# A four-layer graph network in one kernel: a transpose and the setup sums moved from TensorE to VectorE, small products issued in larger batches, and a new order of operations

## The chip, the cores and the metric

The kernel runs on one core of one Trainium2 chip. All times are device microseconds (us) of that core for one execution; the span of a profile, from the first to the last instruction, is some 1.8 us shorter than the time of the same execution (2386.3 against 2388.06 for the changed kernel). The median of several executions is quoted with its lowest and highest value. Of all runs in this study one stray execution (5676.19 us, told below) is left out; all others are fast runs, with mean granted clocks from 0.981 to 0.999.

## The reference

The input is 128 graphs of 64 nodes with 512 features, and one weighted 64x64 adjacency matrix per graph. Everything is fp32. Four layers follow, each a residual around a graph layer with a layer norm and a relu ahead of it. Cut to what matters here:

```python
# layer 0: two hypergraph convolutions; H = (adj != 0)
h  = relu(layernorm(x))
m  = relu(conv(h, H, W1) + b1)              # 512 -> 1024
z  = layernorm(m) * gamma + beta
x  = x + (conv(z, H, W2) + b2) + h          # 1024 -> 512
# layer 1: attention with weight tanh(s_i + s_j), then A @ h @ w
# layer 2: q, k, v; weight = adj * exp(q k^T); x += softmax-like mean of v
h  = relu(layernorm(x))
q, k, v = h @ Wq.T + bq, h @ Wk.T + bk, h @ Wv.T + bv
# layer 3: T = row-normalised adj * exp(leaky_relu(s_j + s_i)); K = 3
h  = relu(layernorm(x))
x  = x + relu(h @ Wk[0] + (T h) @ Wk[1] + (T T h) @ Wk[2] + sum(bk))
```

## The kernel before

Two graphs make a tile of 128 rows, and four tiles make a group. There are 16 groups. All of them pass layers 0 and 1 (the first half), then all pass layers 2 and 3 (the second half), because the weights of both halves use the same two buffers (`wa_mem` and `wb_mem`), which are filled anew in between. Large products use seven instead of eight block products (Strassen).

The kernel is not written in the order in which it runs. Each operation is declared with an engine, a cost and the buffers that it reads and writes. A pass at build time then places the operations one by one: of those that could start first, it takes the one with the smallest priority. It also chooses the buffer slots. The priorities come from about sixty constants, which had been tuned for exactly these operations and costs.

```python
STRETCH, PERIOD1, PERIOD2 = (2.01, 1.52, 3.8, 3.15), 99.32, 100.99
AT = {"x0": -1000.31, "apart": -0.04, "w1": -1140.59, ...}       # cut
...
if pick is not None and (best is None or (t0, pick.prio) < (best[0], best[1].prio)):
    best = t0, pick
assert best and best[0] < float("inf"), "no operation can go on: too few slots"
```

The setup of layer 0 folds gamma, beta and the mean of the second layer norm into W2. `mm` multiplies all of W2 by two columns, and VectorE then subtracts the spread row from W2 so that z needs no mean taken off:

```python
def mm():
    for c in range(KH):
        nc.tensor.matmul(p.t[0:2, :], gsc[:, c, :], w2_sb[:, c, :], start=(c == 0), stop=(c == KH - 1))
...
for c in range(KH):                        # VectorE: W2 * gamma - mean row
    nc.vector.scalar_tensor_tensor(w2_sb[:, c, :], w2_sb[:, c, :], gb2[:, 0, c:c + 1], pm.t,
                                   op0=ALU.mult, op1=ALU.subtract)
```

Layer 0 scales z by its reciprocal deviation only (`rs`), and GpSimd adds h and b2 to x while this goes on:

```python
nc.gpsimd.tensor_add(xx.t, xx.t, h.t)
nc.gpsimd.tensor_add(xx.t, xx.t, b2_b.t)
...
rs = norm_stats(lambda k, z=z: z.t[:, k * D:(k + 1) * D], 2, [(z, 0), (z, 1)])[1]
nc.scalar.activation(half(), half(), AF.Copy, scale=rs.t)
```

Layer 2 issues a batch of 16 small logits products (64 columns, on halves of the array: the form 128*64 in the trace) as soon as one q tile is there. Layer 3 transposes T on TensorE, copies it on ScalarE, multiplies T by T, and applies both to h, one batch of 16 small products for each tile:

```python
def mt():
    for t in range(T):
        nc.tensor.transpose(quad(pt)[:, t, :], tr.t[:, t, :], ident)
pe(KD * TR, mt, trk, [pt])
act(0.59, lambda: nc.scalar.copy(tt.t[:, :, 0, :], quad(pt)), [pt], [(tt, 0)])
def m2():
    for t in range(T):
        nc.tensor.matmul(quad(p2)[:, t, :], tr.t[:, t, :], tt.t[:, t, 0, :], start=True, stop=True)
...
def lm(h=h, pq=pq, t=t):                   # one call per tile
    for c in range(KD):
        for i, half in enumerate(HALVES):
            nc.tensor.matmul(quad(pq[i])[:, c, :], h.t[half, c * P:(c + 1) * P],
                             tt.t[half, t, :, half], start=True, stop=True)
```

## Time and profile before

| | before |
|---|---|
| median of 4 runs | 2400.38 us (2398.42 to 2402.01) |
| span of the profiled run | 2395.1 us |
| TensorE busy / not busy in it | 2356.3 / 38.8 us |
| VectorE, ScalarE, GpSimd busy | 1721.2, 1263.5, 938.2 us |
| stretches at half clock ahead of the last 3 us | 2, of 3.4 us each (clock record of the trace) |

The first line of the table held 3 runs when the prediction was made, with a median of 2401.43 us. "Not busy" is the span less TensorE's busy time. The prediction shows the lines of the page and of the windows from which this is read; what matters in them is that TensorE has no work in only 38.8 us of 2395, of which 16.6 us lie in the first 105 us (the head), 9.9 between 1150 and 1300 us (the change of halves) and nearly all of the rest after that.

### The profile page before, as it was taken

The numbers are of one execution on the slowest core, as the hardware profiler recorded it, in microseconds if no ns is written. First come the engines' busy times: TensorE is split into PE (matmuls) and PEld (weight loads), VectorE is DVE, ScalarE is ACT, GpSimd is POOL, SyncE is SP. The second block draws the span as 40 slices with busy tenths as digits, with TensorE's granted clock in tenths as the row PEclk, the third lists the DMA queues.
The fourth block names the chain that finished last, engine by engine and source line by source line (L and its number), as shares of the span: only waits on it lengthen the run. The fifth ranks groups of instructions, "written<-read, shape, count | busy, mean of one in ns | idle before, by whom it ended". The sixth has DMA issues, their size and how long they took to land.

```text
span 2395.1 us, 33543 instructions
## 1 busy us (share of the span) xinstructions
PE 2356.3 (98%) x11930; PEld 1855.0 (77%) x11930; DVE 1721.2 (72%) x3676; ACT 1263.5 (53%) x1754; POOL 938.2 (39%) x1450
## 2 busy tenths in 40 slices
PE   7999999999999999999999999999999999999999
PEld 3576677776777776777778888888888888888887
DVE  7887878787878787877878556666666666666664
ACT  2666565566565566565745445544445444454431
POOL 5234455434455434455344333333333333333321
PEclk9999999999999999999999999999999999999999
DMA  7232222232223222222532232222322222222211
GB/s 242 54 80 47 65 68 71 68 78 51 65 66 73 67 80 52 61 67 77 146 89 62 66 74 55 69 56 58 78 64 60 66 50 71 73 56 64 52 42 36
DMA packets 335928, 168.78 MB, mean 70 GB/s; under 512 B 284688, under 2 KB 290832, under 8 KB 335760
## 3 DMA queue, kind: packets, MB, share of 16 engines
q1 hardware_dynamic: 335760, 166.63, 28.0%
q8 instruction: 94, 1.54, 0.3%
q14 instruction: 74, 0.61, 0.1%
HBM read 64.76 MB, written 34.70 MB: 42 GB/s over the span
## 4 chain that ended last, share of the span: by engine, by line
PE 84%; DVE 6%; DMA 4%; ACT 2%; POOL 2%; issue 2%; SPq 0%; DVEq 0%; POOLq 0%; ACTq 0%
PE ps L595 60%; PE ps L818 11%; PE ps L534 4%; PE ps L936 2%; PE ps L731 2%; PE ps L879 2%; DVE s_s_vu_tt L869 1%; DMA x<-xm 1%; PE ps L844 1%; ACT o L543 1%; DVE bd L854 1%; ACT h L525 1%; POOL u L867 1%; POOL rs L511 1%; DVE st L508 1%
## 5 line engine op out<-in xcount | busy, mean ns | idle before, releaser
L525 ACT ACTIVATE h<-x,nm,rs 128x512 f32<-128x512 f32 x384 | 307.1, 813 | 456.5 <-POOL nm L518 455.3
L595 PE MATMUL ps<-wb_mem,rT_a 128*128 128x256 f32 x2056 | 476.8, 380 | 1.7 <-DVE z_hT L615 0.9
L595 PEld LDWEIGHTS ps<-wb_mem,rT_a 128*128 128x128 f32 x2056 | 386.5, 190 | 74.8 <-issue 20.3
L510 POOL TENSOR_SCALAR rs<-mv 128x1 f32<-128x1 f32 x320 | 101.5, 317 | 534.2 <-DVE mv L509 452.9
L595 PE MATMUL ps<-wb_mem,s_s_vu_tt 128*128 128x256 f32 x1152 | 275.0, 379 | 0.2 <-DVE s_s_vu_tt L587 0.2
L595 PE MATMUL ps<-wb_mem,tmp_mB_s 128*128 128x256 f32 x1152 | 261.3, 379 | 0.2 <-DVE tmp_mB_s L587 0.2
L595 PEld LDWEIGHTS ps<-wb_mem,s_s_vu_tt 128*128 128x128 f32 x1152 | 218.5, 190 | 43.1 <-issue 10.5
L595 PE MATMUL ps<-wb_mem,mT_a 128*128 128x256 f32 x1016 | 240.7, 380 | 1.8 <-ACT u L563 1.3
L595 PEld LDWEIGHTS ps<-wb_mem,tmp_mB_s 128*128 128x128 f32 x1152 | 217.6, 190 | 29.6 <-DVE tmp_mB_s L587 0.6
L595 PE MATMUL ps<-wa_mem,mT_a 128*128 128x512 f32 x512 | 238.0, 593 | 2.1 <-DVE u L567 2.1
L949 POOL TENSOR_TENSOR u<-u,bk_b 128x256 f32<-128x256 f32 x96 | 76.2, 799 | 352.3 <-DVE u L567 292.6
L511 POOL TENSOR_TENSOR rs<-rs,mhalf 128x1 f32<-128x1 f32 x320 | 202.9, 634 | 26.6
L595 PEld LDWEIGHTS ps<-wb_mem,mT_a 128*128 128x128 f32 x1016 | 190.6, 190 | 28.6 <-ACT u L563 1.5
L508 DVE BATCH_NORM_STATS2 st<-x 128x6 f32<-128x512 f32 x256 | 174.1, 680 | 32.4 <-DMA x<-xm 30.8
L595 PE MATMUL ps<-wa_mem,s_s_vu_tt 128*128 128x512 f32 x384 | 182.9, 599 | 1.0 <-ACT c_b L453 0.6
L595 PEld LDWEIGHTS ps<-wa_mem,mT_a 128*128 128x128 f32 x512 | 96.0, 190 | 105.4 <-issue 92.5
L565 DVE TENSOR_TENSOR u<-ps,u 128x256 f32<-128x256 f32 (+1 forms) x160 | 84.4, 527 | 112.1 <-PE ps L595 84.6
L623 POOL TENSOR_TENSOR u<-u,row_sh_q 128x256 f32<-128x256 f32 x96 | 70.9, 746 | 235.0 <-DVE u L565 205.9
L545 ACT COPY rT_a<-z_hT 128x1024 uint16<-128x1024 uint16 x128 | 144.3, 1161 | 4.4 <-DMA z_hT<-tmp_mB_s 4.2
L534 PEld LDWEIGHTS ps<-bd,h 128*128 128x128 f32 x1024 | 129.0, 192 | 16.1 <-issue 8.6
L707 ACT ACTIVATE z_hT<-z_hT 128x512 f32<-128x512 f32 x128 | 79.8, 625 | 116.7 <-DVE z_hT L615 116.6
L563 ACT COPY u<-ps 128x256 f32<-128x256 f32 (+1 forms) x160 | 72.5, 453 | 129.7 <-PE ps L818 71.5
(172 smaller groups left out, 4317.1 us busy)
## 6 DMA issues: line engine op xcount, KB each, us to landing
x<-in_x_dram SPq DMA_DIRECT2D x64, 256.0 KB, 2.8
xm<-x SPq DMA_DIRECT2D x64, 256.0 KB, 2.0
x<-xm SPq DMA_DIRECT2D x64, 256.0 KB, 2.7
out_dram<-x SPq DMA_DIRECT2D x64, 256.0 KB, 2.2
adj<-in_adj_dram SPq DMA_DIRECT2D x32, 256.0 KB, 4.1
rw<-row SPq DMA_DIRECT2D x96, 64.0 KB, 2.8
wb_mem<-in_Wk_dram SPq DMA_DIRECT2D x6, 512.0 KB, 4.4
wa_mem<-in_W1T_dram SPq DMA_DIRECT2D x2, 1024.0 KB, 5.9
```

What stands on the lines that cost most here:

```text
L508: dve(0.69, lambda i=i: nc.vector.bn_stats(st.t[:, i, :], src(i)), [r[i]], [(st, i)])
L510: pool(0.3, lambda: nc.gpsimd.tensor_scalar_add(rs.t, mv.t[:, 1:2], EPS), [mv], [rs])
L511: pool(0.65, lambda: nc.gpsimd.tensor_tensor(rs.t, rs.t, mhalf, ALU.pow), [rs], [rs])
L525: act(0.82, lambda: nc.scalar.activation(h.t, xx.t, AF.Relu, bias=nm.t, scale=rs.t), [xx, nm, rs], [h])
L534: nc.tensor.matmul(quad(p)[:, c, :], h.t[:, c * P:(c + 1) * P], rhs(), start=True, stop=True)
L545: act(1.16, lambda: nc.scalar.copy(u16(dst()).rearrange("p c (k q) -> p c k q", q=2), u16(back()).rearrange("p (q c r) -> p c r q", q=2, c ...
L563: act(n / 1200 + 0.17, lambda: nc.scalar.copy(at(0)(), p1.t[:, :n]), [p1], [(U, 0)])
L565: dve(c_v(n), lambda: nc.vector.tensor_add(at(1)(), p2.t[:, :n], at(0)()), [p2, (U, 0)], [(U, 1)])
L595: nc.tensor.matmul(p.t[:, :n], lhs()[:, c, :], rhs(c), start=first and c == 0, stop=c == kc - 1, skip_group_check=True)
L707: act(0.63, lambda: nc.scalar.activation(z.t[:, cols], z.t[:, cols], AF.Relu), [(z, j)], [(z, j)])
L818: nc.tensor.matmul(pair(p.t)[:, o, :], a, b, start=first and o == 0 and c == 0, stop=c == 1, skip_group_check=True)
L949: pool(0.88, lambda: nc.gpsimd.tensor_add(U.t[:, iv], U.t[:, u[1]], add()), [u, ka], [v])
```

## The change

Its intent is to take work from TensorE, the engine that is busy 98% of the time, and to issue its smallest products in fewer, larger batches. The parts: (1) VectorE transposes T in blocks of 32x32, so the product that needs T^T has 64 instead of 128 columns; (2) logits are issued for two q tiles at once, and the products with T for two tiles at once; (3) W2 is no longer centred, and what was left of the sums in the setup is done by VectorE, with one product with ones at the end to add over the partitions; ScalarE scales W2 by gamma; (4) z is centred instead, by a bias operand of the same ScalarE operation that scales it, for which GpSimd works out an offset; (5) the layer-3 setup holds fewer temporaries at once, and all priorities are new. The diff cut to its core:

```diff
-    STRETCH, PERIOD1, PERIOD2 = (2.01, 1.52, 3.8, 3.15), 99.32, 100.99
+    STRETCH, PERIOD1, PERIOD2 = (2.14, 5.22, 3.19, 0.39), 82.22, 140.0      # and all of AT
     def setup_l0():
-        pe(c_mm(512, KH), mm, ["gsc0", "gsc1", *wkeys("w2", 0, KH)], [p])   # mm, two spreads,
-        ...                                                                 # W2 * gamma - row
+        for c in range(KH):                                                 # c == 0: tensor_scalar
+                dve(0.77, lambda c=c: nc.vector.scalar_tensor_tensor(
+                    acc.t, w2_sb[:, c, :], gb2[:, 1, c:c + 1], acc.t, op0=ALU.mult, op1=ALU.add), ...)
+        for c in range(KH):
+            act(0.72, lambda c=c: nc.scalar.activation(w2_sb[:, c, :], w2_sb[:, c, :], AF.Copy, scale=gb2[:, 0, c:c + 1]), ...)
+        pe(c_mm(512, 1), lambda: nc.tensor.matmul(pb.t, ones, acc.t, start=True, stop=True), [acc], [pb])
     def setup_l2():                                                         # in the loop over o
-            pe(c_mm(1, KD), mg, [k_, "bq_c"], [pg])
+                dve(0.77, lambda o=o, k_=k_: nc.vector.scalar_tensor_tensor(bk.t, k_.t, bq_c[:, o:o + 1], bk.t, ...), ...)
     ... layer 0
-                    act(0.7, lambda half=half, rs=rs: nc.scalar.activation(half(), half(), AF.Copy, scale=rs.t), ...)
+                nm = offset(mv, rs)
+                    act(0.72, ... nc.scalar.activation(half(), half(), AF.Identity, bias=nm.t, scale=rs.t), ...)
     ... layer 2
+            waiting.append((i, j, q))
+            if len(waiting) < 2:
+                return
     ... layer 3
-                nc.tensor.transpose(quad(pt)[:, t, :], tr.t[:, t, :], ident)
+                    nc.vector.transpose(tt.t[s.start + j * B:s.start + (j + 1) * B, :, 0, i * B:(i + 1) * B],
+                                        tr.t[s.start + i * B:s.start + (i + 1) * B, :, s.start + j * B:s.start + (j + 1) * B])
-                def lm(h=h, pq=pq, t=t):
+            def lm(hh=hh, pqs=pqs, t0=t0):
+                for k in range(2):
```

## The prediction

> **What bounds the kernel now.** I read the page first (busy shares, slices, chain of waits), then windows over the stages, then the timeline of TensorE alone, because the page says that TensorE is busy nearly always and only single records can show where time is still to be had.
>
> ```profile
> PE 2356.3 (98%) x11930; PEld 1855.0 (77%) x11930; DVE 1721.2 (72%) x3676; ACT 1263.5 (53%) x1754; POOL 938.2 (39%) x1450
> ...
> PE 84%; DVE 6%; DMA 4%; ACT 2%; POOL 2%; issue 2%; SPq 0%; DVEq 0%; POOLq 0%; ACTq 0%
> ```
>
> TensorE's busy time is all but 39 us of the 2395 us span, and it is 84% of the chain that ends last. The second engine, VectorE, has a quarter of its time free. So two things count: records taken from TensorE, and idle stretches of TensorE that close. Windows over the stages (columns: busy us of PE, weight loads, DVE, ACT, POOL, then clock, DMA share, GB/s) say where the idle 39 us are:
>
> ```profile
> 0.00:105.00 105.00, 88.41 (x300) 47.78 (x301) 82.93 (x161) 40.65 (x60) 46.49 (x66) 0.98 0.52 161
> 105.00:1150.00 1045.00, 1044.73 (x4395) 755.66 (x4394) 831.97 (x1845) 643.56 (x909) 481.70 (x747) 1.00 0.27 66
> 1150.00:1300.00 150.00, 140.15 (x806) 118.49 (x804) 118.55 (x250) 78.35 (x106) 64.47 (x102) 0.99 0.39 104
> 1300.00:2300.00 1000.00, 994.27 (x5934) 857.60 (x5932) 638.14 (x1320) 476.63 (x646) 326.54 (x508) 1.00 0.27 64
> 2300.00:2396.00 96.00, 88.78 (x503) 75.48 (x501) 49.59 (x103) 24.32 (x35) 18.99 (x28) 0.99 0.13 35
> ```
>
> Head 16.6, first half (layers 0 and 1) 0.3, change of halves 9.9, second half (layers 2 and 3) 5.7, tail 7.2. The first half can get no shorter except by fewer records, and the change takes none from it. In the second half the chain repeats every 73.2 us, one group of four tiles per period (1403.95 to 1477.34 to 1550.53):
>
> ```profile
> 1403.95 13.15 PE ps L595 x60
> ...
> 1477.34 13.15 PE ps L595 x60
> ...
> 1550.53 13.15 PE ps L595 x60
> ```
>
> Within that period the timeline of TensorE shows what the small products cost (start, length, records):
>
> ```profile
> 1467.66 0.66 PE L915 MATMUL ps<-ident,bd 128*128 128x128 f32 x4
> 1468.16 2.82 PE L595 MATMUL ps<-wb_mem,rT_a 128*128 128x256 f32 x12
> ...
> 1474.39 2.95 PE L936 MATMUL ps<-s_s_vu_tt,h 64*128 64x128 f32 x48
> 1477.27 2.86 PE L595 MATMUL ps<-wb_mem,mT_a 128*128 128x256 f32 x12
> ...
> 1502.50 0.69 PE L844 MATMUL ps<-y_qT,z_hT 128*64 128x64 f32 x16
> 1503.12 1.99 PE L818 MATMUL ps<-wa_mem,row_sh_q 128*128 128x256 f32 x8
> 1505.04 0.69 PE L844 MATMUL ps<-y_qT,z_hT 128*64 128x64 f32 x16
> 1505.65 1.99 PE L818 MATMUL ps<-z_hT,wa_mem 128*128 128x256 f32 x8
> 1507.49 1.89 PE L818 MATMUL ps<-wa_mem,row_sh_q 128*128 128x256 f32 x8
> ...
> 1527.08 1.16 PE L936 MATMUL ps<-s_s_vu_tt,h 64*128 64x128 f32 x16
> 1528.17 0.69 PE L844 MATMUL ps<-y_qT,z_hT 128*64 128x64 f32 x16
> ```
>
> Read starts, not lengths. Eight records of 256 columns take 1.73 us from start to start when full-array work stands on both sides (0.216 each), but 1.92 between two logits batches (1503.12 to 1505.04) and 1.84 after one (1505.65 to 1507.49). So a batch costs its own 0.62 us, about 0.09 ahead of it and 0.10 behind: 0.81 us. The product with T (L936) comes already as 48 records in one run and 16 in another, the 16 next to a logits batch.
>
> [...] a 256-column record is listed with 380 ns and starts 216 ns apart. That is why I count starts.
>
> **The change part by part.**
>
> 1. T^T by VectorE. Goes: four transposes per group, 1467.66 to 1468.16, of which 4 x 0.11 = 0.44 us is their own, x 16 groups = 7.0 us of TensorE, on the path that sets the end. Also a 585 ns ACT copy per group. Comes: 8 VectorE block transposes per group of 128 elements per partition. I estimate 0.25 us each, from 0.31 us for the 256-element mask at L668 less something for the shorter row: 2.0 us per group, 32 us in all. VectorE has 638 of 1000 us busy there, so it fits. The following T x T product narrows from 128 to 64 columns: its eight records take 0.89 us, and the 65-column products of L679 are listed at the same 269 against 276 ns, so I give this nothing.
>
> 2. Larger batches. Before, per group: three lone logits batches 3 x 0.81 = 2.43; T product plus logits batch, 1.70 (1527.08 to 1528.78) + 0.20 = 1.90; 48 records, 2.88 + 0.20 = 3.08. Sum 7.41 us. After: two logits batches of 32 (one such run in this trace, 1207.64, takes 1.08) at 1.08 + 0.20 = 1.28, and two T batches of 32 (one at 1272.55 takes 1.99) at 2.19. Sum 6.94. Saved 0.47 x 16 = 7.5 us. The step to notice is that fixing the T product at 32 + 32 gains almost nothing against 48 + 16; the logits give 0.35 per pair, and the lost neighbourhood of logits and T product takes a part of that back.
>
> 3. Setup. The centring product L435 goes: 34.92 to 41.88, 7.0 us. Two row spreads (L439, L440) of 2.1 us become one of 0.86: 1.3 us. The 32 one-column records of L474 (0.81 + 0.81 + 1.77 = 3.4) become 8 (0.9): 2.5 us. Together 10.8 us of TensorE in the head. VectorE loses L443 (5.3) and two tiny copies, and gains seven sums of 0.69 and one of about 0.45 for beta, three and one for the bias: 5.3 + 2.5. About +1 to +2 us net. ACT gains 8 x 0.72 = 5.8 us (duration from L718), early. This is the part where removed TensorE work need not be removed time, as VectorE is 79% busy over the head; but L435 stood directly before the first W1 product (41.88) while W1 had been combined by about 13 us, so I expect most of it to come through.
>
> 4. Centring moves to z. ACT's scaling gets a bias operand, no longer run; POOL makes 64 more offsets of 466 ns, 30 us on an engine that is 39% busy. About half a microsecond more between statistics and z, in a half with 0.3 us of TensorE idle. I give it 0.
>
> 5. The layout: all priorities are new, loads for setup hold fewer temporaries at once. In the head the idle is 9.5 us before the first product, 2.1 behind u, 0.8 for Wk, small pieces. Around 77 us the planes for z wait for temporaries of the layer-3 setup (chain: bk rows land, L500, then the ACT planes). The new order loads the Wq/Wk pieces ahead of W1 and frees temporaries sooner. I estimate head idle 16.6 to 11 (-6), change of halves 9.9 to 6 (-4), tail 7.2 to 6 (-1), second half 5.7 to 4 (-2): 13 us of 39.
>
> Sum: 7.0 + 7.5 + 10.8 + 13 = 38 us, the removed records at full value; what of the 10.8 us in the head turns into idle is the risk that rival (b) holds. 2401.4 - 38 is 2363 us, 1.6% less.
>
> **The rivals.** (a) The waits move: T^T now needs a chain of VectorE blocks before the product, batches need two q tiles out of two slots, and a pair of T products takes four PSUM banks at once. For it: the 5.7 us that are idle in the second half are such waits already (L879 behind L882, 4.6 us). Against it: 64% VectorE and many independent products to fill with. If it costs 0.7 us per group, 11 us come back: 2373. (b) The head is bound by VectorE and transfers, and the 10.8 us of TensorE work there turn into idle, with little idle closed: 2401 - 15 - 7 = 2379. For it: VectorE at 16.9 to 19.7 us of each 20 between 40 and 100 us. (c) The new layout closes nearly all that can be closed (head to 8, change to 2, tail to 5): another 9 to 12 us off, 2351. Against it: the first load and the last store can't be hidden. (d) VectorE becomes the bound of the second half: no, 64% + 3%.
>
> **Range and chances.** Between (b) with a part of (a), 2380, and (c) with adjacent T batches, 2346. Faster by over 2% means below 2353.4, 48 us off, which needs (c) nearly whole: 0.23. Slower by over 2% would need idle that nothing in the profile suggests: 0.01.
>
> **What would show it.** Period of the second half 72.3 us against 73.2 (0.44 + 0.47 off); no transposes on TensorE; two runs of logits of 32 records and two of T products per group; period of the first half unchanged at 71.8 (271.38 to 343.14); head window of 105 us holding about 10 us more of finished group work; PE busy near 2331. Wrong would be: idle before the T product or the logits (rival a), VectorE filled and TensorE idle in the first 100 us (rival b), or the change of halves as long as before.

## The result, and the profile after

The changed kernel takes 2387.24 us (median of 4 runs, 2385.84 to 2388.33) against 2400.38: 13.1 us or 0.55% less. Ratios here and below are the mean time of one kernel's fast runs over that of the other's in the same rounds, so they are not quite the ratio of the medians quoted; this one is 0.9945, with a 95% interval of 0.9928 to 0.9963. The verdict is "same" at 2%, as the larger chance of the prediction said, but the time is above its range of 2346 to 2380.

The page of the changed kernel, busy times and chain of waits:

```profile
PE 2332.2 (98%) x11824; PEld 1849.8 (78%) x11824; DVE 1751.3 (73%) x3804; ACT 1269.8 (53%) x1745; POOL 976.2 (41%) x1514
...
PE 88%; DVE 4%; DMA 3%; ACT 1%; SPq 0%; issue 0%; POOL 0%; DVEq 0%; ACTq 0%; POOLq 0%
```

TensorE's busy time is 24.1 us less, at 2332.2, where the prediction had said "near 2331". But the span of this run is 2386.3 us, only 8.8 less than the 2395.1 of before (that run of before was on its fast side). So TensorE now has 54.1 us without work, 15.3 more than before. The windows, with the same columns as in the prediction, say where:

```profile
0.00:105.00 105.00, 81.03 (x261) 45.70 (x262) 86.68 (x162) 51.08 (x72) 52.34 (x71) 0.97 0.59 181
105.00:1150.00 1045.00, 1044.03 (x4396) 756.33 (x4395) 827.16 (x1846) 654.20 (x904) 517.80 (x805) 1.00 0.29 66
1150.00:1300.00 150.00, 137.47 (x763) 115.47 (x762) 114.65 (x250) 78.27 (x105) 61.33 (x102) 0.98 0.42 102
1300.00:2300.00 1000.00, 994.81 (x5999) 866.90 (x5998) 679.12 (x1451) 465.37 (x636) 329.74 (x513) 1.00 0.28 64
2300.00:2386.30 86.30, 74.90 (x411) 65.37 (x409) 43.73 (x98) 20.94 (x31) 14.96 (x24) 0.95 0.12 33
```

Length less TensorE's busy time, after and before: head 24.0 against 16.6 (+7.4), first half 1.0 against 0.3, change of halves 12.5 against 9.9 (+2.7), second half 5.2 against 5.7, tail 11.4 against 6.3 to the end of the span (+5.1). The steady stretches are as good as before; the new idle time is in the head, the change and the tail.

**The second half.** The chain of waits of the changed kernel (start, length, what) shows its period over two groups:

```profile
1406.97 18.33 PE ps L593 x84
...
1550.77 18.33 PE ps L593 x84
```

Two groups take 143.80 us, 71.9 each, against 73.3 before (146.58 for two; the prediction took 73.2, the second of its two periods): 1.39 us less per group, 22 us over 16. The prediction had said 0.91. TensorE's timeline shows the reason:

```profile
1403.13 3.84 PE L948 MATMUL ps<-s_s_vu_tt,h 64*128 64x128 f32 x64
1406.90 2.86 PE L593 MATMUL ps<-wb_mem,mT_a 128*128 128x256 f32 x12
...
1433.86 1.15 PE L850 MATMUL ps<-y_qT,z_hT 128*64 128x64 f32 x32
1434.94 1.99 PE L817 MATMUL ps<-z_hT,wa_mem 128*128 128x256 f32 x8
```

The two batches of 32 products with T (L948) run as one of 64: 3.77 us from start to start, and what full-array work beside a half-array batch loses, about 0.20 us, is lost once instead of twice. From start to start, twelve records of 256 columns take 2.69 us ahead of a batch with T (kernel before, 1524.39) and 2.70 behind one (1406.90), against 2.59 elsewhere; eight take 1.82 ahead of a logits batch (1432.04) and 1.83 behind one (1434.94), against 1.73. So a group spends 3.97 on them and 2 x 1.28 on the logits (L850), 6.53 in all, against 7.41 before: 0.88 us less, 14 us over 16 groups, where the prediction had 7.5. With the transposes (0.44) and the product T x T, now of 64 columns (0.83 us for its eight records in place of 0.89), that makes 1.38 of the 1.39 us.

**The tail.** TensorE's timeline where the last group's T is needed (the bracket is the idle time ahead and what ended it):

```profile
2338.14 1.97 PE L932 MATMUL ps<-s_s_vu_tt,bd 128*128 128x64 f32 x8 [6.79 <-DVE s_s_vu_tt L923]
2340.56 5.13 PE L948 MATMUL ps<-s_s_vu_tt,h 64*128 64x128 f32 x64 [0.46 <-ACT s_s_vu_tt L934]
2345.63 2.86 PE L593 MATMUL ps<-wb_mem,rT_a 128*128 128x256 f32 x12
```

TensorE waits 6.79 us for VectorE's transposes. Of the 16 groups only three make it wait for them at all, 9.6 us together; in the others, products of other parts fill the time, and in the last group there are none left. VectorE's timeline shows the chain itself:

```profile
2335.56 2.52 DVE L923 STREAM_TRANSPOSE s_s_vu_tt<-bd 32x128 f32<-32x128 f32 x8
```

Eight transposes one after the other take 2.5 us of the 6.8. What follows the wait is slow too: the 64 products take 5.07 us from start to start instead of 3.77, and the eight of L932 last 1.97 instead of 1.00 (at 1400.37 us). The window over these 8 us shows the clock that goes with it, in the third column from the end:

```profile
2338.00:2346.00 8.00, 7.40 (x74) 7.07 (x75) 1.03 (x2) 3.50 (x7) 0.00 (x0) 0.67 0.01 2
```

The granted clock is 0.67 on average after the wait; between 2346 and 2352 us it is 1.00 again. So the products behind the wait of 6.8 us take another 2.3 us (0.97 + 1.30). The clock record of the trace holds only full and half clock, and its half-clock stretches are 3.4 or 6.8 us long. Before the last few us of the run there are two of them before the change, at 46.2 and 1264.7 us, 6.8 us together, and after it stretches at 66.6, 87.1, 1268.1 and 2336.5 us, of 3.4, 3.4, 6.8 and 6.8 us, 20.4 us together. In the 3.4 us ahead of them TensorE had worked 2.71 and 1.52 us before the change, and 0.79, 0.70, 1.46 and 0.00 us after it; the longest single waits ahead of those at 66.6 and 87.1 us were 2.61 and 3.24 us. Most of the stretches thus follow time without work, but the one at 46.2 us follows 3.4 us of which 2.71 were busy, so these traces do not show what sets them off. Records in them last up to about twice as long: besides the eight of L932, eight of L593 last 3.41 us at 66.96 against 1.89 at 79.44. From these two I estimate that up to half of the added 13.6 us, 6.8 us, was lost in this way.

**The head.** The VectorE timeline of the changed kernel around the first Strassen product with W2, and the GpSimd timeline beside it:

```profile
74.74 0.68 DVE L585 TENSOR_TENSOR s_s_vu_tt<-rT_a 128x512 f32<-128x512 f32 x1
75.46 1.65 DVE L585 TENSOR_TENSOR s_s_vu_tt<-s_s_vu_tt,rT_a 128x512 f32<-128x512 f32 x1
77.02 1.75 DVE L585 TENSOR_TENSOR rT_a<-rT_a 128x512 f32<-128x512 f32 x1
78.70 1.75 DVE L585 TENSOR_TENSOR s_s_vu_tt<-rT_a,s_s_vu_tt 128x512 f32<-128x512 f32 x1
```

```profile
75.02 1.54 POOL L694 TENSOR_TENSOR x<-x,h 128x512 f32<-128x512 f32 x1 [3.02 <-ACT h L523]
76.63 1.60 POOL L695 TENSOR_TENSOR x<-x,row_sh_q 128x512 f32<-128x512 f32 x1
78.19 1.72 POOL L694 TENSOR_TENSOR x<-x,h 128x512 f32<-128x512 f32 x1
```

The first of four equal VectorE additions takes 0.68 us; the other three take 1.65 to 1.75. Add start and length: they end at 77.11, 78.77 and 80.45 us, and the GpSimd additions (x+h and x+b2) at 76.56, 78.23 and 79.91. Each VectorE addition ends some 0.55 us after a GpSimd one, as if it had waited for that to end and only then done its own work (GpSimd's lengths are the rough ones of the two). The same four additions took 0.68 to 0.69 each in the kernel before (at 90.81 us), where GpSimd was not in the way. What holds VectorE up beside GpSimd the trace does not show; pool_light below tests that it is GpSimd's additions. Between 60 and 100 us this lengthens VectorE's work by about 7 us, against 0.8 before (durations above those of the same form elsewhere, summed). Before 60 us the same sum is 5.4 us, against 7.5 before the change; so over the whole head it is 12.4 against 8.4 us. The change adds about 4 us of it, and most of it now comes late in the head. From 73.79 to 86.35 us the chain of waits of the changed kernel names no engine but VectorE. A little later TensorE pays for it, in its own timeline:

```profile
86.40 3.14 PE L593 MATMUL ps<-wb_mem,rT_a 128*128 128x256 f32 x8 [3.24 <-DVE u L565]
```

### The profile page after: what moved, and what is told of

Read it like the earlier page. It is cut to its first block, busy times and chain, and to the rows that moved or that the text cites. A ratio compares the mean times of both kernels' runs of the same rounds, so it can differ in the third digit from the quotient of the medians.

```text
span 2386.3 us, 33454 instructions
## 1 busy us (share of the span) xinstructions
PE 2332.2 (98%) x11824; PEld 1849.8 (78%) x11824; DVE 1751.3 (73%) x3804; ACT 1269.8 (53%) x1745; POOL 976.2 (41%) x1514
## 3 DMA queue, kind: packets, MB, share of 16 engines
q8 instruction: 93, 1.52, 0.3%
## 4 chain that ended last, share of the span: by engine, by line
PE 88%; DVE 4%; DMA 3%; ACT 1%; SPq 0%; issue 0%; POOL 0%; DVEq 0%; ACTq 0%; POOLq 0%
PE ps L593 61%; PE ps L817 14%; PE ps L532 5%; PE ps L886 2%; PE ps L730 2%; DMA x<-xm 1%; PE ps L948 1%; PE ps L850 1%; DMA rw<-row 1%; DVE st L502 0%; DVE tmp_mB_s L585 0%; PE ps L677 0%; PE ps L932 0%; DVE o L373 0%; SPq L542 0%
## 5 line engine op out<-in xcount | busy, mean ns | idle before, releaser
L523 ACT ACTIVATE h<-x,nm,rs 128x512 f32<-128x512 f32 x384 | 300.7, 810 | 404.9 <-POOL nm L510 387.3
L593 PE MATMUL ps<-wb_mem,rT_a 128*128 128x256 f32 x2056 | 475.0, 382 | 5.1 <-DVE u L565 3.2
L593 PEld LDWEIGHTS ps<-wb_mem,rT_a 128*128 128x128 f32 x2056 | 390.1, 191 | 73.0 <-issue 10.0
L593 PE MATMUL ps<-wb_mem,s_s_vu_tt 128*128 128x256 f32 x1152 | 275.7, 380 | 1.4 <-DVE x L772 0.5
L593 PE MATMUL ps<-wb_mem,tmp_mB_s 128*128 128x256 f32 x1152 | 262.4, 380 | 3.2 <-DVE tmp_mB_s L585 3.2
L593 PEld LDWEIGHTS ps<-wb_mem,s_s_vu_tt 128*128 128x128 f32 x1152 | 215.6, 190 | 56.2 <-issue 24.4
L593 PEld LDWEIGHTS ps<-wb_mem,tmp_mB_s 128*128 128x128 f32 x1152 | 218.5, 190 | 35.2 <-DVE tmp_mB_s L585 6.0
L593 PE MATMUL ps<-wb_mem,mT_a 128*128 128x256 f32 x1016 | 242.6, 380 | 0.0
L593 PE MATMUL ps<-wa_mem,mT_a 128*128 128x512 f32 x512 | 236.8, 594 | 2.6 <-DVE u L565 2.6
L593 PEld LDWEIGHTS ps<-wb_mem,mT_a 128*128 128x128 f32 x1016 | 191.2, 190 | 32.0 <-issue 7.4
L505 POOL TENSOR_TENSOR rs<-rs,mhalf 128x1 f32<-128x1 f32 x320 | 193.7, 605 | 26.7
L593 PE MATMUL ps<-wa_mem,s_s_vu_tt 128*128 128x512 f32 x384 | 180.4, 593 | 1.6 <-DVE s_s_vu_tt L585 0.9
L593 PEld LDWEIGHTS ps<-wa_mem,mT_a 128*128 128x128 f32 x512 | 95.9, 190 | 104.7 <-issue 95.3
L561 ACT COPY u<-ps 128x256 f32<-128x256 f32 (+1 forms) x160 | 72.3, 452 | 188.5 <-PE ps L817 123.1
L510 POOL TENSOR_SCALAR nm<-mv,rs 128x1 f32<-128x1 f32 x320 | 146.2, 457 | 31.2
L621 POOL TENSOR_TENSOR u<-u,row_sh_q 128x256 f32<-128x256 f32 x96 | 77.3, 820 | 185.3 <-DVE u L563 182.1
```

Source lines behind the costliest of these rows:

```text
L505: pool(0.65, lambda: nc.gpsimd.tensor_tensor(rs.t, rs.t, mhalf, ALU.pow), [rs], [rs])
L510: pool(0.47, lambda: nc.gpsimd.tensor_scalar(nm.t, mv.t[:, 0:1], rs.t, -1.0, op0=ALU.mult, op1=ALU.mult), [mv, rs], [nm])
L523: act(0.82, lambda: nc.scalar.activation(h.t, xx.t, AF.Relu, bias=nm.t, scale=rs.t), [xx, nm, rs], [h])
L593: nc.tensor.matmul(p.t[:, :n], lhs()[:, c, :], rhs(c), start=first and c == 0, stop=c == kc - 1, skip_group_check=True)
```

## The experiments

Two things can be read from the result. One theory is that the parts themselves give back what they save: the transposes are a chain on VectorE that TensorE must wait for, and VectorE bounds the head, where the setup sums were put. The rival is that the parts are fine and the new order is poor, or that the order alone made the 13 us. A third, for the head, is that GpSimd or the transfers bound it and not the moved sums.

A difficulty runs through all of this. Where an operation is added or its cost changes, the ordering pass gives another order of the whole kernel. The first four kernels have that fault. I could not try everything either: the logits batches alone under the old priorities, and the changed kernel with the old layer-3 setup, could not be placed at all ("too few slots") and never ran, so nothing of them is on record. From the fifth kernel on I kept the declared operations and costs and changed only what is issued, so that the order stays the same, wherever that was possible. Single traces also differ by themselves: tt_same_order below leaves the first half as it was, and its trace has 19.9 us without work in the head where the kernel before has 16.6. A difference of some 3 us in one stretch of one trace shows nothing.

### z_offset: the offset on z alone, in the kernel before

```diff
-                rs = norm_stats(..., 2, [(z, 0), (z, 1)])[1]
+                mv, rs = norm_stats(..., 2, [(z, 0), (z, 1)])
+                nm = offset(mv, rs)                        # one GpSimd operation, 0.47 us
-                    act(0.7, ... nc.scalar.activation(half(), half(), AF.Copy, scale=rs.t), ...)
+                    act(0.72, ... nc.scalar.activation(half(), half(), AF.Identity, bias=nm.t, scale=rs.t), ...)
```

> The kernel before with one part of the change alone: the scaling of z gets a bias operand, so GpSimd computes 64 more offsets (466 ns each) and every z waits for one more small operation. Everything else, the layout too, as before. Theory of the prediction (part 4, worth 0): 2400 us within 3. Theory L (the layout is laid out so tightly that a half microsecond more in the z chain shifts the order of everything behind it): idle of TensorE appears in every group of the first half, some 3 to 4 us per group, 2440 to 2460 us.

Measured: 2477.29 us (2474.78 to 2480.45) against 2398.69 for before on the same chip, ratio 1.0328 (1.0309 to 1.0348). That is above both expected ranges: a part to which the prediction gave 0 costs 79 us. The loss is in the first half, as the windows and then the waits of TensorE (in total, times, longest) show:

```profile
105.00:1150.00 1045.00, 1001.52 (x4108) 717.36 (x4108) 791.66 (x1733) 611.64 (x851) 494.32 (x755) 0.98 0.24 62
```

```profile
PE ps L538 <- ACT bd L686: 31.4, 10, 3.7
```

TensorE has 43.5 us without work in a stretch where it had 0.3, the clock is 0.98 in it instead of 1.00, and the largest wait is at another place than the one changed. Fourteen half-clock stretches lie ahead of the last few us of this trace, 71.7 us in all (the mean granted clock of that run is 0.986, against 0.998 before). That looks like a bad order rather than like the latency of one offset, and the run offset_same_order below tests it.

### setup_sums: the offset and the setup sums, in the kernel before

The edit is the diff of z_offset plus the parts of the change in the setup of layers 0 and 2 (beta and bias sums on VectorE, W2 scaled by ScalarE), with the layer-3 setup of before.

> The kernel before with the whole setup part alone (W2 not centred, sums on VectorE, offset on z), in the layout of before. TensorE has 10.8 us of work less. Prediction: 2390 us (10.8 us come through). Rival b (VectorE and transfers bound the head): PE busy falls by about 10 us and the time by under 3. Theory L: as the offset alone, 2430 to 2460, less at most 10.

Measured: 2485.12 us (2481.56 to 2486.33), ratio 1.0358 (1.0342 to 1.0374). The proper comparison is with z_offset on the same chip: 7.8 us slower, although TensorE's busy time is 4.9 us less (2382.2 against 2387.1). In the first 105 us TensorE is busy 81.75 us against 87.86 there: the time without work in the head rose by 6.1 us. Taking 10.8 us of TensorE work from the head made the kernel no faster. The order was derived anew in both, so this is a first sign and no proof.

### tt_vector: only the transposes by VectorE, in the kernel before

```diff
-                nc.tensor.transpose(quad(pt)[:, t, :], tr.t[:, t, :], ident)
+                    nc.vector.transpose(tt.t[...], tr.t[...])             # as in the change
-        act(0.59, lambda: nc.scalar.copy(tt.t[:, :, 0, :], quad(pt)), [pt], [(tt, 0)])
```

> The kernel before with T^T by VectorE alone, layout of before. TensorE loses 64 transposes, 7.0 us. Prediction: 2393 us. Rival a (the wait for eight VectorE blocks takes the place of the transposes): the T product waits for VectorE about 1 us per group or more, and 6 to 8 us at the last group where nothing is left to fill with; 2400 to 2415 us.

Measured: 2417.20 us (2414.26 to 2423.52), ratio 1.0081 (1.0060 to 1.0102). It is 0.8% slower ("same" at 2%) and just above the range of rival (a), with TensorE busy 2361.2 us. TensorE waits for the transposes in two groups, 5.4 us together. Again the order is another one, so that the size says little.

### dead_product: the removed W2 product put back into the changed kernel, its result unused

```diff
-        acc, pb = Buf("o"), Buf("ps")
+        acc, pb, dead = Buf("o"), Buf("ps"), Buf("ps")
+        def mm():
+            for c in range(KH):
+                nc.tensor.matmul(dead.t[0:2, :], gb2[:, :, c], w2_sb[:, c, :], start=(c == 0), stop=(c == KH - 1))
+        pe(c_mm(512, KH), mm, ["gb2g", "gb2b", *wkeys("w2", 0, KH)], [dead])
```

> The changed kernel with the removed product of W2 (16 records of 512 columns, 7 us of TensorE) put back in the head as dead work that nobody reads, all else the same. If the removed 7 us came through as time (prediction, step 3), the time goes up by 6 to 8 us to 2394. If the head is bound by VectorE and transfers (rival b), the dead work lies in what is now idle: within 3 us of 2387, idle of the first 105 us down by about 5 or more.

Measured: 2390.06 us (2388.52 to 2395.78, 5 runs), ratio to before 0.9968 (0.9953 to 0.9983). By the medians that is 2.8 us above the changed kernel, by the two ratios 0.0023 or 5.5 us, and the intervals overlap. In the head TensorE is busy 89.76 us instead of 81.03, so nearly all of the product fell into time without work there. But the order moved too, and the first half of that trace has 8.3 us without work instead of 1.0. By itself the run is inconclusive: somewhere between 0 and 7 us.

### offset_same_order: the offset on z, in the kernel before, with its order kept

The offset is issued inside the declared operation that takes the power, so the pass places the same operations with the same costs:

```diff
+        if off:
+            nm = Buf("nm")
+            def both():
+                nc.gpsimd.tensor_tensor(rs.t, rs.t, mhalf, ALU.pow)
+                nc.gpsimd.tensor_scalar(nm.t, mv.t[:, 0:1], rs.t, -1.0, op0=ALU.mult, op1=ALU.mult)
+            pool(0.65, both, [rs, mv], [rs, nm])
+            return nm, rs
```

> The kernel before, with the 64 GpSimd offsets and the biased scaling of z put in without letting the kernel's ordering pass see them: every engine keeps the instruction order of before, and only the instructions themselves are there. The same work in the run z_offset cost 77 us. Theory order (the 77 us come from another order of the instructions, not from half a microsecond more before each z): 2400 us within 5. Theory latency (the wait itself costs): 2440 us or more.

Measured: 2402.74 us (12 runs, 2397.76 to 2406.45) against 2399.82 (31 runs) for before, ratio 1.0013 (1.0003 to 1.0023). The window of the first half:

```profile
105.00:1150.00 1045.00, 1043.69 (x4390) 754.63 (x4389) 833.77 (x1840) 653.96 (x910) 508.85 (x806) 1.00 0.26 67
```

TensorE is busy all but 1.3 us there. So the offset itself costs about 3 us, and the other 76 us of z_offset were the order that the old priorities give once the operation is declared. The new priorities are a necessary part of this change, not an extra.

### tt_same_order: the transposes by VectorE, in the kernel before, with its order kept

The eight block transposes are issued in the place of the TensorE transposes in the declared order, and the ScalarE copy is left empty. The product T x T and its copy narrow to 64 columns, as in the change (not shown in the cut). The ordering pass does not know of VectorE's new work here, so the order was not made for it.

```diff
-            for t in range(T):
-                nc.tensor.transpose(quad(pt)[:, t, :], tr.t[:, t, :], ident)
+            for s in HALVES: ...
+                        nc.vector.transpose(tt.t[..., 0, ...], tr.t[...])
-        act(0.59, lambda: nc.scalar.copy(tt.t[:, :, 0, :], quad(pt)), [pt], [(tt, 0)])
+        act(0.59, lambda: None, [pt], [(tt, 0)])
```

> The kernel before, with T^T by eight VectorE block transposes per group in place of four TensorE transposes and one copy, in the order of before. PE busy falls by about 10 us. Prediction, step 1: 2393 us (7.0 us off). Rival a: the T product now waits for 2.5 us of VectorE in place of 0.4 us of TensorE plus 0.6 of copy; what TensorE gives back is lost in that wait, 2398 to 2408 us.

Measured: 2404.37 us (20 runs, 2398.07 to 2407.55), ratio 1.0015 (1.0007 to 1.0022). The second half and the tail of it:

```profile
1300.00:2300.00 1000.00, 991.92 (x5907) 854.33 (x5906) 667.58 (x1443) 469.95 (x638) 328.54 (x513) 1.00 0.28 64
2300.00:2405.70 105.70, 95.00 (x530) 80.78 (x528) 57.70 (x120) 24.79 (x35) 20.75 (x30) 1.00 0.12 32
```

The four transposes per group are gone from TensorE, and its busy time fell by 3.9 us (2352.4 against 2356.3). But it lacks work for 14.5 us in the change of halves instead of 9.9, for 8.1 us in the second half instead of 5.7 and for 10.7 us in the tail instead of 6.3 (the profiled execution is the slowest of the 20, and its head has 3.3 us more, which are not the edit's). The part saves nothing; it costs about 4 us. This is rival (a) in effect: a wait takes the place of the work. But it is not the product with T^T that waits: TensorE's list of waits has none for it. In the last group the eight transposes stand in VectorE's queue ahead of the end of a Strassen combination (`u`), and TensorE waits for that:

```profile
2350.93 2.51 DVE L919 STREAM_TRANSPOSE s_s_vu_tt<-bd 32x128 f32<-32x128 f32 x8
2353.47 0.42 DVE L567 TENSOR_TENSOR u<-ps,u 128x256 f32<-128x256 f32 x1
```

```profile
2353.95 2.86 PE L595 MATMUL ps<-wb_mem,rT_a 128*128 128x256 f32 x12 [3.37 <-DVE u L567]
```

In the first group they stand ahead of a q tile in the same way, and the logits wait 2.6 and 2.0 us.

### head_light: the changed kernel with ten dots and ten sums of the setup cut to a few elements

```diff
-                    acc.t, w2_sb[:, c, :], gb2[:, 1, c:c + 1], acc.t, ...)
+                    acc.t[:, :8], w2_sb[:, c, :8], gb2[:, 1, c:c + 1], acc.t[:, :8], ...)
-                dot(lambda wv=wv: wv.t, lambda av=av: av.t, ...)         # and the bias sums, bv dots
+                light(lambda wv=wv: wv.t, ...)                           # copies one column
```

It is wrong on purpose (the error still falls within the tolerance of the comparison). Declared costs and order are unchanged.

> The changed kernel in its own order, with VectorE's setup sums of the head (ten dot products of layer 3, seven sums for beta, three for the bias) shortened to tiny instructions: about 13 us of VectorE taken out, nothing of TensorE. Wrong result on purpose. If VectorE bounds the head (rival b), the time falls by 4 to 10 us and TensorE's idle in the first 105 us from 24 to 16 or less. If transfers or the z chain bound it: within 2 us of 2387.

Measured: 2379.83 us (2375.04 to 2381.04), ratio 0.9908 (0.9888 to 0.9928), by the ratios 0.0037 or 9 us below the changed kernel, by the medians 7.4. The head:

```profile
0.00:105.00 105.00, 87.37 (x296) 51.61 (x297) 80.72 (x163) 56.32 (x79) 49.83 (x72) 0.98 0.58 181
```

TensorE's time without work there falls from 24.0 to 17.6 us when VectorE is relieved. The transfers are the same (DMA share 0.58 against 0.59), so they do not explain the 6.4 us.

### pool_light: the changed kernel with GpSimd's x+h and x+b2 cut to 8 columns

```diff
-                pool(1.43, ... nc.gpsimd.tensor_add(xx.t, xx.t, h.t), ...)
-                pool(1.39, ... nc.gpsimd.tensor_add(xx.t, xx.t, b2_b.t), ...)
+                pool(1.43, ... nc.gpsimd.tensor_add(xx.t[:, :8], xx.t[:, :8], h.t[:, :8]), ...)
+                pool(1.39, ... nc.gpsimd.tensor_add(xx.t[:, :8], xx.t[:, :8], b2_b.t[:, :8]), ...)
```

It is wrong on purpose (relative error 0.16), with the order unchanged.

> The changed kernel in its own order, with the two GpSimd additions into x per tile (x + h, x + b2) cut to 8 columns. Wrong result on purpose. In the trace of the changed kernel VectorE's additions take 1.65 us in place of 0.69 where these GpSimd additions run beside them, 7 us of such lengthening between 60 and 100 us. If that lengthening is part of what holds the head: 2 to 6 us faster, VectorE's long additions gone. If not: within 2 us.

Measured: 2377.71 us (2376.64 to 2378.36), ratio 0.9906 (0.9891 to 0.9920), 9 us below the changed kernel. The head, and the four additions from above:

```profile
0.00:105.00 105.00, 88.51 (x297) 53.27 (x298) 82.06 (x174) 55.87 (x79) 34.99 (x72) 0.97 0.58 181
```

```profile
69.90 0.68 DVE L585 TENSOR_TENSOR s_s_vu_tt<-rT_a 128x512 f32<-128x512 f32 x1
70.61 0.69 DVE L585 TENSOR_TENSOR s_s_vu_tt<-s_s_vu_tt,rT_a 128x512 f32<-128x512 f32 x1
```

The additions last 0.68 to 0.69 us again, come 5 us earlier, and the head has 16.5 us without work instead of 24.0. Relieving GpSimd helps the head as much as relieving VectorE of its sums. The trace says how: the lengthening of VectorE's work in the head is 0.7 us here instead of 12.4, and the wait of 3.24 us at 86.40 is gone. Half of the lead comes earlier than the additions shown: the product that started at 61.23 us in the changed kernel starts at 57.48 here, after a stretch in which GpSimd's first additions are cut too. And since the kernel before had 8.4 us of this lengthening, the 9 us are not what the change added. GpSimd itself was busy only 52.34 of 105 us; whether its own queue delayed something besides was not tested. What the reduced additions are worth in the rest of the kernel cannot be told apart from this run, but the steady windows hardly moved (1043.75 and 995.61 us busy, against 1044.03 and 994.81).

### sums_on_tensor: the changed kernel with the sums of beta and of the bias back on TensorE

W2 is still not centred, and the priorities are those of the changed kernel. One W2 product of 16 records replaces the eight VectorE operations for beta, and the one-column products of before replace the four for the bias.

```diff
+        def mm():
+            for c in range(KH):
+                nc.tensor.matmul(p.t[0:2, :], gb2[:, :, c], w2_sb[:, c, :], start=(c == 0), stop=(c == KH - 1))
+        pe(c_mm(512, KH), mm, ["gb2g", "gb2b", *wkeys("w2", 0, KH)], [p])
-                dve(0.77, ... scalar_tensor_tensor(acc.t, w2_sb[:, c, :], gb2[:, 1, c:c + 1], acc.t, ...), ...)
+            pe(c_mm(1, KD), mg, [k_, "bq_c"], [pg])
-                dve(0.77, ... scalar_tensor_tensor(bk.t, k_.t, bq_c[:, o:o + 1], bk.t, ...), ...)
```

> The changed kernel with the beta row and the bias column computed on TensorE again as before (10 us of TensorE, 8 us of VectorE less); W2 still not centred, priorities of the changed kernel. If the head is bound by VectorE (head_light: 13 us of VectorE out gave 7 us), the 10 us of TensorE cost nothing and the 8 us of VectorE give 3 to 5 us: 2380 to 2386. By the prediction (TensorE bounds): 2397.

Measured: 2382.15 us, the median of three fast runs from 2380.74 to 2382.40; a stray of 5676.19 is not among them (with it the median is 2382.27). The ratio to before is 0.9921 (0.9905 to 0.9938), 0.0024 or 6 us below the changed kernel; the intervals just overlap (0.9928 to 0.9938). The result is correct. The head:

```profile
0.00:105.00 105.00, 88.51 (x296) 49.07 (x297) 81.53 (x154) 46.86 (x68) 53.64 (x75) 0.97 0.56 176
```

This is the clearest run on part 3: TensorE is busy 9.4 us longer in all (2341.6 against 2332.2), and the kernel is not slower but faster by some 5 us, since it has 15.1 us less without work. Of these 7.5 are in the head, which is back at 16.5 us, as in the kernel before; 4.6 are in the change of halves and 2.2 in the second half, where nothing was edited. The order is not quite the same (operations were exchanged), but the priorities are, and the head moves in the same direction and by the same 7 us as in the two runs whose order was kept.

### tt_light: the changed kernel with one copy in place of four block transposes

```diff
-            for i in range(2):
-                for j in range(2):
-                    nc.vector.transpose(tt.t[...], tr.t[...])
+            nc.vector.tensor_copy(tt.t[s, :, 0, :], tr.t[s, :, s])
```

It is wrong on purpose (T is not transposed, though the error stays within the tolerance). The order is unchanged; the serial chain per group is two operations instead of eight.

> The changed kernel in its own order, with one plain VectorE copy per half in place of four block transposes (about 1.9 us of VectorE less per group, 30 us in all). Wrong result on purpose. If the transposes on VectorE cost time only where nothing is left to fill with (the first and the last group), 2 to 5 us faster; if they are what holds the second half, 10 us or more; if nothing, within 1 us. The wait of the last T product falls from 6.8 to about 5.

Measured: 2378.56 us (2376.64 to 2381.67), ratio 0.9909 (0.9894 to 0.9924): 8.7 us below the changed kernel by the medians, and between the two sizes expected. The second half, and the last T product:

```profile
1300.00:2300.00 1000.00, 997.31 (x6019) 869.53 (x6018) 656.30 (x1368) 460.60 (x629) 333.20 (x515) 1.00 0.27 63
```

```profile
2326.08 1.97 PE L929 MATMUL ps<-s_s_vu_tt,bd 128*128 128x64 f32 x8 [4.88 <-DVE s_s_vu_tt L921]
```

TensorE has 2.7 us without work in the second half instead of 5.2, and 9.5 in the tail instead of 11.4; the last wait is 4.88 instead of 6.79 us. VectorE is busy 23 us less in the second half. TensorE's busy time is also 4.2 us less (2328.0 against 2332.2) with the same records, and the trace has 13.7 us at half clock instead of 20.4; about half of those 6.7 us, 3.4 us, would be the clock's part (an estimate from this one trace). So the length of the transposes costs the changed kernel up to 9 us, but most of the last wait remains: it is the chain ahead of the transposes, and there is nothing else left for TensorE to do.

### same_parts_other_order: the changed kernel with other priorities

Nothing but the constants differs. They come from a search by random steps on what the ordering pass reckons.

> The changed kernel with all its parts and another set of priorities, found by many small random steps from its own towards a shorter planned time under late transfers. If the order that came with the change left much on the table (prediction, step 5, took 13 us of idle away): 2377 or less. If the order is about as good as these parts allow: within 4 us of 2387.

Measured: 2386.15 us (2385.17 to 2387.29), ratio 0.9939 (0.9922 to 0.9955), the same as the changed kernel. A second set of priorities, reached by steps from the first and so not independent of it, ends at the same time. That speaks weakly against the rival that the order which came with the change is poor for its parts.

### sums_back_and_last_tt: the sums back on TensorE, and TensorE's transpose in the last group only

The edit is that of sums_on_tensor, with new priorities, and:

```diff
+        if g == NG - 1:
+            pt = Buf("ps")
+            ...
+            pe(KD * TR, mt, trk, [pt])                     # transposes on TensorE
+        else:
             for i, s in enumerate(HALVES):
                 dve(1.2, lambda s=s: blocks(s), [(tr, s.start)], [(tt, 2 + i)])
```

> The changed kernel with both sums back on TensorE, T^T of the last group alone by TensorE, and priorities stepped in the same way for this set of parts. VectorE-bound head: head idle below 17 us (24 before this edit) and 2374 to 2381 us, the fastest correct kernel of the study. If TensorE work is what counts, 2390 or more.

Measured: 2376.80 us (2374.57 to 2377.09), ratio 0.9898 (0.9884 to 0.9913). It is correct and the fastest kernel of the study that is: 10.4 us below the changed kernel by the medians, 1.0% below before. TensorE is busy 93.83 of the first 105 us, so it has 11.2 us without work there, the number to which the prediction had expected the change to bring it, and 9.8 in the tail. Three things differ here, so the run shows that the reading of the parts is useful, not what each is worth.

## Why the prediction was right or wrong

The prediction had the verdict (within 2%) right, and which records leave TensorE, and the time wrong: 2363 said, 2387.24 measured, 7 us outside the range. What failed is its account of the waits: it took the removed work at full value and had TensorE's time without work fall by 13 us; that time rose by 15.3 us. By its own steps:

1. **T^T by VectorE, 7.0 us: wrong.** The records are gone from TensorE, but the gain is not there. With the order kept, the part alone costs about 4 us (tt_same_order): the transposes hold up VectorE's queue, and TensorE waits for what stands behind them. In the order of the change the T product itself waits, 9.6 us in three groups. One transpose, over 32 partitions of 128 elements each, takes 302 ns (median of 128 in the trace of the changed kernel), not the 250 estimated: 38.7 us of VectorE in all, and 2.5 us in a chain per group. Without most of that chain the changed kernel is 8.7 us faster. This is rival (a), to which the prediction gave 11 us only as an alternative.
2. **Larger batches, 7.5 us: right in kind, too small.** It is 14 us (0.88 per group), because the two batches with T run as one of 64 products. The period of 71.9 us (1.39 less) is better than the 72.3 predicted.
3. **Setup, 10.8 us "at full value": wrong.** The work left TensorE, and the time without work in the head grew by 7.4 us, with VectorE busy 86.68 of 105 us. Three runs show why, each by one other relief: fewer sums on VectorE, no GpSimd additions in its way, or the sums back on TensorE; each brings the head back to 16.5 to 17.6 us. The prediction named the reason itself ("VectorE is 79% busy over the head") and still expected "most of it to come through". It did not see that GpSimd's additions lengthen VectorE's work, by 12.4 us in the head after the change and by 8.4 already before it.
4. **Centring on z, 0: nearly right.** The offset costs about 3 us with the order kept. That declaring it under the old priorities costs 79 us was not foreseen; the new priorities of the change pay for it.
5. **Layout, 13 us of idle time closed: wrong, and the largest miss.** It is 15.3 us more instead of 13 less, a miss of 28 us. Head 24.0 instead of 11, change of halves 12.5 instead of 6, tail 11.4 instead of about 6. These 15.3 us contain the waits of points 1 and 3, so the points are not to be added up. The new order repairs what the parts disturb; it did not also close what had been idle before.

The sum, by the trace: 7.0 + 14 + 10.8 = 31.8 us of TensorE work removed; 15.3 us more without work; and an estimated 6.8 us of slower work in the half-clock stretches above. That makes 31.8 - 15.3 - 6.8 = 9.7 us, against 8.8 us between the two profiled spans and 13.1 between the medians. TensorE's busy time, 24.1 us lower, is the first less the last (25.0). "PE busy near 2331" was thus right partly by luck: the extra gain from the batches hid the slower work at half clock, which the prediction had left out.

Of the rivals, (b) describes the head as it is, and (a) the tail and T products; both happened, and their times (2379 and 2373) were each too low; put together by the prediction's own numbers (16 and 10 us over 2363) they give 2389. (c) did not happen. (d), VectorE as the bound of the second half, is refuted for the steady state (TensorE 994.81 us of 1000).

What stays open: what made the change of halves 2.7 us worse, which no run singled out (in TensorE's list of waits there, the logits stand out: 3.6 us behind q tiles against 1.3 before, which would be the other half of rival (a); in sums_on_tensor they wait 1.6 us, and the whole stretch has 7.9 us without work); and how much the two halves of part 3, the beta and the bias sums, count for by themselves.

## What to carry to other kernels

Work taken from the busiest engine counts only in the stages where that engine sets the end: look at each stage by itself, and ask which engine receives the work and what it waits for or collides with there: here 10.8 us of work left TensorE in the head, and its time without work there rose by 7.4 us. Look at the granted clock behind a long wait too: here it was 0.67 over the 8 us behind a wait of 6.79 us, and the products there took 2.3 us more. Where operations are ordered by a tuned pass, test a part with the order kept, since otherwise one measures the order: here 3 us looked like 79.
